# Scatters without fills between them, and a denser timetable, in the first layer of a two-layer graph transformer

## The chip, the cores and the metric

The kernel runs on one core of a Trainium2 chip. The metric is the device time of one launch in microseconds, the median of several runs. The profile shows one execution, taken by the hardware profiler. The core's engines work side by side, each through its own instructions in order: TensorE (PE, with its weight loads PEld), VectorE (DVE), ScalarE (ACT), GpSimd (POOL) and SyncE (SP, which here issues transfers).

## The reference, cut to what matters

Two layers, each a graph part, an attention part and an expert part, on 3125 nodes of 256 features with 50,000 edges sorted by `dst`. Everything is float32. The change lies in layer 0; the graph part of layer 0 is

```python
def _L0_gnn_ref(input, edge_index, edge_weight, weight, bias):
    support = jnp.matmul(input, weight)
    row, col = (edge_index[0], edge_index[1])
    msgs = support[col] * edge_weight[:, None]
    output = jax.ops.segment_sum(msgs, row, num_segments=input.shape[0])
    return output + bias
...
xn = _layernorm(x, axis=-1)
x = x + _L0_gnn_ref(xn, edge_index, edge_weight, ...) + _L0_mix_ref(xn[None], ...)[0]
x = x + _L0_ffn_ref(_layernorm(x, axis=-1)[None], ...)[0]
```

`_L0_mix_ref` is a linear attention over all nodes. `_L0_ffn_ref` sends each node through a shared network and through two of eight experts, which the largest two of eight router values choose. Layer 1 ends in an expert part whose weights come from a second graph, 2048 rows with 32,768 edges; the kernel sorts those edges by their second end, and half of that sort is done during layer 0.

## The kernel before

**The graph part as a matrix.** The kernel doesn't gather rows per edge. It builds a dense weighted adjacency matrix in the chip's main memory (tile `adj`, 25 blocks of 128 rows, one row per `dst`, and 3200 columns, one per `src`, float32) and multiplies it on TensorE with the supports `sup`. Building it takes three steps:
- *Fills of zeros* (`fill`, L471): 25 transfers of 1.6 MB from SP.
- *Chunks* (`edge_chunk`, L384 to L426): the edges come in 16 chunks of 8, 12, ten times 32, 16, 16, 12 and 7 lots; a lot is 128 edges, one per partition. On DVE a chunk adds up weights of edges that fall on one place and works out each edge's place (`ch_code`, `ch_same`, `ch_prod`, `ch_sum`, `ch_place`).
- *Scatters* (`edge_scatter`, L438): one indirect transfer from POOL per lot, 391 in all, 128 single floats each.

**The runs.** Six runs of adjacency matmuls (L599; `RUNS`, blocks 0-3, 4-7, 8-11, 12-15, 16-19, 20-22) each go over 14 groups of columns of `gT`, with 4 or 3 blocks each; DVE adds the result to `gT` (L605; in the first run ACT copies it, L603). SP loads a run's blocks (`load`, L568), in two halves; a load waits until the lots of its edges have landed and until the buffer of the run before is free. Then gT is transposed and added to `x` (L624, L627), and the last two blocks (`CLOSING`, L643, L646) are multiplied chunk by chunk of nodes, beside the moments of the next layer norm (L228 to L239), its rows on ACT (L243), their transposes (L250) and the router's product (L281).

**The sort.** DVE, ACT and PE work on the second graph's sort beside all this (`sort_by_low`): first a ranking by digits (L1344 to L1393), then 256 *columns*: for each, DVE and ACT make selection matrices (`s_hot`, `we`/`wc`/`wi`, `s_z`: L1456 to L1468) and PE multiplies them (L1484, L1489). Where they stand in the engines' order is up to the layer's program: two per group of a run (`ranked(2)`), any number in the pauses of `until`, and what is left is spread evenly over the 27 steps of the transposes and the closing blocks (`columns`).

**The timetable.** PE, DVE, ACT and SP run in the order in which the program writes their instructions. That order comes from a clock of the program's own, `now`, which `advance(us)` moves on by estimates. Three places read it:

```python
yield RATE * (ENDS[c] + (ENDS[c + 1] - ENDS[c]) * i / STEPS) / 128 - AHEAD   # a chunk's step is due
while self.pending and (22.0 + PACE * self.released - LEAD <= until or ...)  # a lot is handed to POOL
ready = 38.0 + RATE * min(16 * (b0 + n) + 4, NJ)                             # a run may start
until(ready)                                                                 # until then: columns of the sort
```

`RATE` (L59) and `PACE` (L60) are the microseconds that the timetable gives to a lot. A lot that is handed over waits for the latest instruction of the tokens or runs at that place in the program (`self.mark`).

**The scatters on POOL.** `spaced` (L294) puts the scatters into one order: each scatter of an edge lot, and later each of the 50 scatters of the expert part's rows into `slots` (L1127), comes behind a `memset` of a small tile `idle` (L298), which itself comes behind the scatter before it. Nothing reads `idle`. `turn_on_queue` states an order on POOL's queue alone, without a semaphore of its own.

Of the kernel before, what the change touches and what calls it, by code (L numbers as in the profile page):

```python
# [9 lines left out]
F32 = mybir.dt.float32  # L10
# [45 lines left out]
SW = 264  # L56
STEPS = 5
AHEAD = 90.0
RATE = 1.38  # L59
PACE, LEAD = 1.48, 78.0  # L60


E2, EC = 32768, 256
# [17 lines left out]
def scatter(nc, table, idx, rows, add=False):  # L81
    kw = {"compute_op": OP.add} if add else {}
    return nc.gpsimd.indirect_dma_start(  # L83
        out=table, out_offset=bass.IndirectOffsetOnAxis(ap=idx, axis=0),
        in_=rows, in_offset=None, **kw)


def pieces_of(c):

    return min(NT, (ENDS[c + 1] + DRIFT) // (16 * P) + 1)  # L90
# [11 lines left out]
def held(t):  # L102

    return P if t < NT - 1 else REST
# [31 lines left out]
class Kernel:  # L136
# [8 lines left out]
    def constants(self):  # L145
        nc, a, c = self.nc, self.a, self.const
        self.x = c.tile([P, NT, D], F32, name="x")
        nc.vector.memset(self.x[:, NT - 1, :], 0.0)
        self.ident = c.tile([128, 128], F32, name="ident")
        make_identity(nc, self.ident)  # L150

        self.above = c.tile([128, 128], F32, name="above")
        nc.gpsimd.memset(self.above, 1.0)
        nc.gpsimd.affine_select(out=self.above, in_=self.above, compare_op=OP.is_gt, fill=0.0,
                                base=0, pattern=[[1, 128]], channel_multiplier=-1)
        self.full = c.tile([128, 128], F32, name="full")
        nc.vector.memset(self.full, 1.0)

        self.node = c.tile([128, EC], F32, name="node")
        nc.gpsimd.iota(self.node, pattern=[[1, EC]], base=0, channel_multiplier=0,  # L160
                       allow_small_or_imprecise_dtypes=True)
        self.real = c.tile([128, 1], F32, name="real")
        nc.gpsimd.memset(self.real, 1.0)
        nc.gpsimd.affine_select(out=self.real, in_=self.real, compare_op=OP.is_gt, fill=0.0,
                                base=REST, pattern=[[0, 1]], channel_multiplier=-1)
        self.idle = c.tile([128, 128], F32, name="idle")
        self.spacer = None
        self.eps = c.tile([128, 1], F32, name="eps")
        nc.vector.memset(self.eps, LN_EPS)

# [120 lines left out]
        self.tc.add_manual_dep(ins.ins, name, mybir.DependencyInfo(  # L291
            mybir.DependencyClass.NoSync, mybir.DependencyReason.DATA), reason="turns on the queue")

    def spaced(self, ins):  # L294

        if self.spacer is not None:
            self.turn_on_queue(ins, self.spacer)
        rest = self.nc.gpsimd.memset(self.idle, 0.0)  # L298
        self.turn_on_queue(rest, ins.ins.name)
        self.spacer = rest.ins.name  # L300
        return ins

    def unordered(self, group, ins):
# [134 lines left out]
    def edge_scatter(self, c, place, wsum, f):  # L438

        ready = pieces_of(c)  # L440
        ins = self.spaced(scatter(self.nc, self.adj[:], place[:, f:f + 1], wsum[:, f:f + 1]))
        for i in range(ready):
            self.after(ins, self.fills[i], "zeros below")
        self.tc.declare_no_dep(ins.ins, group="adj read", reason="blocks that are complete")
        for i in range(ready, NT):
            self.tc.declare_no_dep(ins.ins, group=f"zeros {i}", reason="rows behind the chunk's")
        for i in range(c + 1):
            self.tc.declare_no_dep(ins.ins, group=f"edges {i}", reason="places of their own")
        self.tc.add_to_no_dep_group(f"edges {c}", ins.ins)
        self.edge_scatters.setdefault(c, []).append(ins.ins)  # L450
        return ins


    def layer0(self):
        nc, tc, a = self.nc, self.tc, self.a
        with ExitStack() as c:
# [43 lines left out]
            def chunks():  # L500
                for c in range(len(WIDTHS)):
                    steps = self.edge_chunk(ed, c)
                    for i in range(STEPS):
                        yield RATE * (ENDS[c] + (ENDS[c + 1] - ENDS[c]) * i / STEPS) / 128 - AHEAD
                        next(steps, None)
# [73 lines left out]
            def until(us):  # L579
                while now < us:  # L580
                    advance(next(sort, 1.0))

            turn = 0
            for b0, n in RUNS:
                ready = 38.0 + RATE * min(16 * (b0 + n) + 4, NJ)
                until(ready)
# [337 lines left out]
    def layer0_ffn(self, arrive, far, sorting):  # L924
        nc, tc, a = self.nc, self.tc, self.a
        NE, FC = 8, 8
        SB = BLK // 128
        with ExitStack() as c:
# [5 lines left out]
            rows = rp.enter_context(tc.tile_pool(name="f0r", bufs=1)).tile([P, NT, SW], F32, name="rows")  # L934
# [77 lines left out]
            def routes():  # L1012
# [95 lines left out]
                abi = big.tile([P, 2, NT], I32, name="abi")  # L1108
# [15 lines left out]
                for t in range(NT):  # L1124
                    p = held(t)
                    for i in range(2):
                        self.unordered("slots", self.spaced(scatter(nc, self.slots[:], abi[:p, i, t:t + 1], rows[:p, t, :])))  # L1127

            kp = c.enter_context(tc.tile_pool(name="f0k", bufs=1))
            ranks = self.sort_by_high(kp, hp) if sorting else iter(())  # L1130
            steps = chain(routes(), self.segments(kp) if sorting else (), ranks)
            output(*first_hidden)
            pending = second_hidden
# [17 lines left out]
            def block_in(b):  # L1151
                n = lots(b)
                e = nc.sync.value_load(exi[0:1, b:b + 1], min_val=0, max_val=NE - 1)
                w1 = wa.tile([128, 2, FC * 128], F32, name="w1")
                b1 = wp.tile([128, FC], F32, name="b1", bufs=3)
                b2 = wp.tile([128, D], F32, name="b2r", bufs=3)
                r = wp.tile([128, SB, SW], F32, name="srow", bufs=3)
                nc.sync.dma_start(r[:, :n, :], self.slots[slot(b):slot(b) + 128 * n, :].rearrange("(i p) w -> p i w", p=128))
                nc.sync.dma_start(w1, a["L0_ffn_W1p"][bass.ds(e, 1)].rearrange("o (k p) f -> p (o k) f", p=128))
                nc.sync.dma_start(b1, self.b1p[bass.ds(e, 1)].rearrange("o p f -> p (o f)"))  # L1160
                nc.sync.dma_start(b2, self.b2[bass.ds(e, 1)].to_broadcast([128, D]))
                return e, w1, b1, b2, r
# [67 lines left out]
            ins = {b: block_in(b) for b in T[:2]}  # L1230
# [1454 lines left out]
```

## Time and profile before

| what | value |
|---|---|
| median of 3 runs | 2459.14 us (2455.91 to 2460.01) |
| the profiled execution | 2454.27 us, span 2452.5 us |
| mean granted clock of TensorE | 0.901 |
| busy: PE, DVE, ACT, POOL | 2001.3, 1472.7, 835.4, 1562.2 us |
| edge scatters (L83, `adj`) | 391, 416.4 us, mean 1065 ns |
| slot scatters (L83, `slots`) | 50, 58.9 us, mean 1178 ns |
| memsets of `idle` (L298) | 441, 99.2 us, mean 225 ns |
| adjacency matmuls (L599 into `pb` and `pc`) | 484 and 160 records, 195.6 and 65.6 us |

The span is the time from the first to the last instruction; the time of the launch is 1.8 us longer. The profiled execution is 4.9 us below the median. Busy times say how much an engine did, not whether others waited for it; a share of the whole span mixes stretches with different limits, and layer 0's graph part takes only the first 755 us of it. Idle time in a row is charged to what ended the wait.

### The profile page before, as it was taken

What the parts mean: (1) busy time and instruction counts of PE and PEld (TensorE: products, weight loads), DVE (VectorE), ACT (ScalarE), POOL (GpSimd) and SP (SyncE); (2) the same over time, 40 slices, a digit from 0 to 9 for tenths busy, and PEclk for the clock granted to TensorE, in tenths of its full rate; (3) what the DMA queues carried; (4) which work ended last, traced back from release to release, by engine and by line L of the source; (5) the groups of instructions that cost most, each with busy time, mean ns of one, the idle gap of its engine ahead of it and who ended that gap; (6) DMA issues with size and microseconds to landing.
All of it is one profiled execution on the core that took longest, in us unless ns stands there. A gap on an engine that the chain in (4) does not pass through costs nothing.

```text
span 2452.5 us, 27755 instructions
## 1 busy us (share of the span) xinstructions
PE 2001.3 (82%) x8319; PEld 1415.0 (58%) x8319; DVE 1472.7 (60%) x3952; ACT 835.4 (34%) x1852; POOL 1562.2 (64%) x1924
## 2 busy tenths in 40 slices
PE   1666699899889989899999547777769779999955
PEld 0444355445555668789999435545546566677634
DVE  6888948986823696122222458898886962233346
ACT  1353144564513112333434323444430142222314
POOL 5888888886000562777777157777776437777742
PEclk9985799899957999999999779999989869999977
DMA  8613538223001125677887432222222112113242
GB/s 270 225 57 111 223 137 273 71 100 108 12 1 35 66 82 171 205 256 245 261 258 239 130 82 55 57 54 56 55 60 47 34 28 38 28 21 81 58 140 68
DMA packets 200603, 275.75 MB, mean 112 GB/s; under 512 B 58562, under 2 KB 159415, under 8 KB 200443
## 3 DMA queue, kind: packets, MB, share of 16 engines
q1 hardware_dynamic: 146815, 224.49, 27.4%
q0 software_dynamic: 48480, 44.59, 8.8%
q10 hardware_dynamic: 5148, 4.80, 0.7%
q8 instruction: 68, 1.11, 0.2%
q14 instruction: 92, 0.75, 0.1%
HBM read 195.35 MB, written 78.42 MB: 112 GB/s over the span
## 4 chain that ended last, share of the span: by engine, by line
PE 59%; DVE 24%; issue 5%; ACT 5%; DMA 5%; POOL 2%; ACTq 0%; DVEq 0%; SPq 0%; POOLq 0%
PE pb L1207 8%; PE pb L599 7%; PE pc L1219 7%; PE fph L1987 7%; PE fpy L2003 7%; DVE v L1748 3%; PE pc L599 3%; PE pw L1754 2%; PE pb L972 2%; PE pc L985 2%; PE pb L281 2%; PE pb L643 2%; DMA g<-tab,t_src 1%; POOL g L76 1%; PE pc L1484 1%
## 5 line engine op out<-in xcount | busy, mean ns | idle before, releaser
L76 POOL DMA_INDIRECT g<-tab,t_src x391 | 377.3, 965 | 198.1 <-issue 151.1
L83 POOL DMA_INDIRECT adj<-ch_sum,ch_place x391 | 416.4, 1065 | 91.9 <-issue 54.3
L83 POOL DMA_INDIRECT sorted<-src,pos x256 | 245.2, 958 | 134.9 <-issue 102.1
L76 POOL DMA_INDIRECT G<-tabg,g_src x256 | 256.9, 1003 | 78.0 <-DMA G<-tabg,g_src 39.3
L1754 PE MATMUL pw<-v,hot 128*128 128x260 f32 x782 | 215.1, 436 | 0.0
L1207 PE MATMUL pb<-xs,w 128*128 128x128 f32 (+1 forms) x1248 | 205.5, 324 | 9.2 <-issue 8.6
L599 PE MATMUL pb<-adj,sup 128*128 128x448 f32 (+1 forms) x484 | 195.6, 549 | 15.1 <-DVE r_tot L1354 13.6
L1207 PEld LDWEIGHTS pb<-xs,w 128*128 128x128 f32 x1248 | 187.7, 194 | 25.8 <-issue 9.6
L1219 PE MATMUL pc<-w,h 128*128 128x256 f32 x896 | 199.7, 379 | 0.0
L1209 ACT ACTIVATE h<-pb,b 128x128 f32<-128x128 f32 (+1 forms) x312 | 129.1, 414 | 176.2 <-PE pb L1207 106.9
L1754 PEld LDWEIGHTS pw<-v,hot 128*128 128x128 f32 x782 | 165.7, 217 | 30.0
L1219 PEld LDWEIGHTS pc<-w,h 128*128 128x128 f32 x896 | 167.3, 190 | 21.2
L2003 PE MATMUL fpy<-fw,fh 128*128 128x256 f32 (+1 forms) x800 | 177.7, 379 | 0.0
L1987 PE MATMUL fph<-xT,fw 128*128 128x512 f32 (+2 forms) x448 | 174.1, 542 | 0.0
L83 POOL DMA_INDIRECT slots<-rows,abi x50 | 58.9, 1178 | 177.8 <-DVE abi L1110 167.9
L2003 PEld LDWEIGHTS fpy<-fw,fh 128*128 128x128 f32 (+1 forms) x800 | 149.6, 187 | 31.8 <-issue 8.5
L1466 ACT ACTIVATE s_z<-s_y,s_val 128x128 f16<-128x128 f16 x256 | 112.4, 486 | 122.6 <-issue 108.2
L1989 ACT ACTIVATE fh<-fph,cols 128x512 f32<-128x512 f32 (+2 forms) x112 | 70.2, 633 | 215.6 <-PE fph L1987 215.6
L599 PEld LDWEIGHTS pb<-adj,sup 128*128 128x128 f32 x484 | 90.0, 193 | 91.8 <-issue 85.5
L1987 PEld LDWEIGHTS fph<-xT,fw 128*128 128x128 f32 x448 | 85.3, 191 | 76.0 <-issue 54.9
L1748 DVE TENSOR_TENSOR v<-msg,own_bank 128x2048 f32<-128x2048 f32 (+2 forms) x50 | 111.9, 2239 | 1.7
L298 POOL MEMSET idle<- 128x128 f32 x441 | 99.2, 225 | 0.3
(591 smaller groups left out, 3674.9 us busy)
## 6 DMA issues: line engine op xcount, KB each, us to landing
adj<-zero SPq DMA_DIRECT2D x25, 1600.0 KB
w<-in_L_ffn_W1p_dram SPq DMA_DIRECT2D x39, 1024.0 KB
w<-in_L_ffn_W2p_dram SPq DMA_DIRECT2D x39, 1024.0 KB
adj<-adj SPq DMA_DIRECT2D x24, 896.0 KB
adj<-adj SPq DMA_DIRECT2D x24, 704.0 KB
slots<-empty SPq DMA_DIRECT2D x1, 7392.0 KB
adj<-ch_sum,ch_place POOLq DMA_INDIRECT x391
g<-tab,t_src POOLq DMA_INDIRECT x391
```

The source lines that it names most:

```text
L76: return nc.gpsimd.indirect_dma_start(out=out, out_offset=None, in_=table, in_offset=bass.IndirectOffsetOnAxis(ap=idx, axis=0))
L83: return nc.gpsimd.indirect_dma_start(out=table, out_offset=bass.IndirectOffsetOnAxis(ap=idx, axis=0), in_=rows, in_offset=None, **kw)
L298: rest = self.nc.gpsimd.memset(self.idle, 0.0)
L599: nc.tensor.matmul(pm[:, :w], sup[:, b, k * 128:(k + 1) * 128], mats[b, h][:, c0 - PARTS[h][0]:c0 - PARTS[h][0] + w], start=(b == b0), sto ...
L1207: nc.tensor.matmul(ph[:, :m], w1[:, k, f * 128:(f + 1) * 128], xs[:, k, :m], start=(k == 0), stop=(k == 1))
L1209: ins = nc.scalar.activation(h[:, f, :m], ph[:, :m], AF.Gelu, bias=b1[:, f:f + 1])
L1219: nc.tensor.matmul(py, h[:, f, i * 128:(i + 1) * 128], w2[:, f, :], start=(f == 0), stop=(f == FC - 1))
L1466: nc.scalar.activation(z[:, i, k, :], y, AF.Relu, bias=val[:, k, s], scale=val[:, 2 + k, s])
L1748: self.latest = nc.vector.tensor_mul(v[:, :n, :, :HD], o[:, :n, None, :HD].to_broadcast([128, n, 4, HD]), weight[:, :n, :, None].to_broadc ...
L1754: nc.tensor.matmul(pw.rearrange("p h c -> p (h c)"), hot[:, k, :], v[:, k, :, :].rearrange("p h c -> p (h c)"), start=(k == 0), stop=(k == ...
L1987: nc.tensor.matmul(ph[:, :m], w1[:, k, f * 128:(f + 1) * 128], xT[:, k, t0 * P:t0 * P + m], start=(k == 0), stop=(k == 1))
L2003: nc.tensor.matmul(py[:p], hs[:, f, i * P:i * P + p], w2[:, f, :], start=(f == 0), stop=(f == FC - 1))
```

## The change

`spaced` becomes `in_turn`: the scatters keep the same order, each behind the one before it, but no `memset` stands between them. The tile `idle` goes. `RATE` falls from 1.38 to 1.22 and `PACE` from 1.48 to 1.27. Line numbers below the edit fall by up to three.

```diff
-RATE = 1.38
-PACE, LEAD = 1.48, 78.0
+RATE = 1.22
+PACE, LEAD = 1.27, 78.0
...
-        self.idle = c.tile([128, 128], F32, name="idle")
-        self.spacer = None
+        self.last_lot = None
...
-    def spaced(self, ins):
-
-        if self.spacer is not None:
-            self.turn_on_queue(ins, self.spacer)
-        rest = self.nc.gpsimd.memset(self.idle, 0.0)
-        self.turn_on_queue(rest, ins.ins.name)
-        self.spacer = rest.ins.name
+    def in_turn(self, ins):
+
+        if self.last_lot is not None:
+            self.turn_on_queue(ins, self.last_lot)
+        self.last_lot = ins.ins.name
         return ins
...
-        ins = self.spaced(scatter(self.nc, self.adj[:], place[:, f:f + 1], wsum[:, f:f + 1]))
+        ins = self.in_turn(scatter(self.nc, self.adj[:], place[:, f:f + 1], wsum[:, f:f + 1]))
...
-                        self.unordered("slots", self.spaced(scatter(nc, self.slots[:], abi[:p, i, t:t + 1], rows[:p, t, :])))
+                        self.unordered("slots", self.in_turn(scatter(nc, self.slots[:], abi[:p, i, t:t + 1], rows[:p, t, :])))
```

## The prediction, made before the changed kernel was run

> **What bounds the kernel now.** I read the page first, then the stretches of layer 0 by time, POOL's timeline, the chain of waits, and last the two programs' instruction orders, a listing without times. On the page:
>
> ```profile
> span 2452.5 us, 27755 instructions
> ...
> PE 2001.3 (82%) x8319; PEld 1415.0 (58%) x8319; DVE 1472.7 (60%) x3952; ACT 835.4 (34%) x1852; POOL 1562.2 (64%) x1924
> ...
> POOL 5888888886000562777777157777776437777742
> PEclk9985799899957999999999779999989869999977
> ```
>
> A digit of the last two rows is 61 us. POOL is dense until 600 us and then empty until 822: that is the edge scatters' end. Nothing there waits for it directly, so I cut layer 0 into stretches (columns: PE, PEld, DVE, ACT, POOL busy; PEclk, DMA share, GB/s):
>
> ```profile
> 424.70:459.30 34.60, 24.19 (x163) 12.45 (x161) 34.49 (x127) 30.64 (x79) 31.10 (x42) 0.86 0.31 112
> 511.80:541.90 30.10, 25.64 (x169) 13.41 (x167) 30.06 (x127) 28.78 (x74) 26.77 (x41) 1.00 0.37 128
> ...
> 631.20:655.40 24.20, 18.56 (x146) 12.92 (x145) 24.19 (x85) 16.10 (x41) 2.31 (x7) 1.00 0.04 13
> 655.40:674.40 19.00, 16.60 (x82) 8.84 (x80) 17.91 (x71) 7.21 (x19) 0.00 (x0) 1.00 0.00 0
> 674.40:755.20 80.80, 64.86 (x219) 44.19 (x220) 18.77 (x60) 15.79 (x34) 0.00 (x0) 0.53 0.08 26
> ```
>
> The first two are the pauses of `until(ready)` ahead of runs 3 and 4 (numbered from 0): DVE is full, making sort columns, while the adjacency matmuls stand still. The third is the transposes of gT, full on DVE too. The last is the closing blocks: DVE busy 18.8 of 80.8 us, TensorE at a granted 0.53. This loop sets its pace (chain of waits):
>
> ```profile
> 676.53 0.48 ACT xT L952
> ...
> 677.05 3.58 PE pc L281 x16
> 680.63 4.50 PE pb L643 x8
> 685.13 0.54 PE pc L1484 x2
> 685.67 4.32 PE pb L643 x8
> ...
> 690.01 0.69 DVE x L646
> ```
>
> After 690.01 come the moments on DVE and the rows on ACT, and at 695.98 L281 again: one lap in 18.9 us. Whatever DVE does between L646 and the moments lengthens the lap.
>
> **The fills.** With and, further on, without one behind it, a scatter looks so on POOL:
>
> ```profile
> 519.80 0.96 POOL L83 DMA_INDIRECT adj<-ch_sum,ch_place  x1 [0.17 <-issue]
> 520.77 0.22 POOL L298 MEMSET idle<- 128x128 f32 x1
> 521.15 0.96 POOL L83 DMA_INDIRECT adj<-ch_sum,ch_place  x1 [0.17 <-DVE wc L1459]
> ...
> 1107.59 0.96 POOL L83 DMA_INDIRECT sorted<-src,pos  x1 [0.30 <-issue]
> 1108.85 0.96 POOL L83 DMA_INDIRECT sorted<-src,pos  x1 [0.30 <-ACT h L1209]
> ```
>
> The step is 1.35 us with the fill and 1.26 without: the fill's 0.22 goes, the gap grows from 0.17 to 0.30, and 0.09 is won, not the 0.39 that fill and gap take. From 39.8 us on 383 lots went in 559 us, 1.46 each, because many scatters last longer than 0.96. So I expect about 1.37, against a timetable that drops by 0.16 (RATE) and 0.21 (PACE). The 391st lot ends at 599.1 - 383 x 0.09 = 565. Lot 340, the last that run 4 needs, ended at 524.1 (counted along POOL's timeline); 332 x 0.09 = 30 us less is 494. The longer scatters sit in the pauses:
>
> ```profile
> L83 POOL DMA_INDIRECT adj<-ch_sum,ch_place x21 | 26.4, 1256 | 3.5 <-issue 1.3 <-DVE s_z L1468 0.8 <-DVE wi L1459 0.5
> ...
> L83 POOL DMA_INDIRECT adj<-ch_sum,ch_place x38 | 38.2, 1004 | 7.3 <-issue 4.4 <-DVE s_z L1468 1.0 <-DVE wc L1459 0.5
> ```
>
> The upper row is the first pause (424.7 to 459.3), the lower one run 3 (459.3 to 511.8): 1256 ns beside sort columns, 1004 beside matmuls. If the pauses go, the lots keep closer to 1.27 and lot 340 comes up to 9 us sooner, at 485. I take 490. The Trainium skill, SBUF — State Buffer, "Who interferes with whom", says that a VectorE instruction in a two-port mode and GpSimd exclude each other for a whole instruction; it speaks against a table set at 1.27, and for lots that quicken once the columns are moved behind them. By it alone lot 340 would be at 485, by the row's mean at 494; the sum below would shift by no more than 5 us.
>
> The slot scatters (L1127, 822 to 902 us) win 50 x 0.09 = 4.5 us on POOL. What ends last there is DVE's d_cum chain, which runs to 915 and lets PE go on; I cost this edit at 0 to -2.
>
> **The timetable.** `ready` is 38 + RATE x (16 x blocks + 4): for runs 3, 4 and 5 it falls from 396, 485 and 551 to 355, 433 and 492. Counting the sort columns (10 DVE instructions for four) between the runs in the two orders:
> - pause before run 3: 53 before, 2 after; before run 4: 51 and 15; before run 5: 12 and 2;
> - transposes: 26 and 76; closing: 12 and 62.
>
> So 100 columns leave the pauses and come back behind the runs. Four take 2.34 us on DVE (519.80 onwards, L1456 to L1468 repeating), 0.586 each.
>
> *Runs.* Run 2 ended at 424.7. In the new order one chunk of 32 lots more (10 us of DVE: L402 3.4, L407 1.5, L411 1.5, L418 2.7, small ones 1) stands ahead of run 1. DVE idled 12.6 us there, at 317.8 "<-PE pb L599", and some of the token stage is full, so I take +5. Run 3 starts at 430 instead of 459.3, lasts 51, then 13 columns beyond the running ones at 0.586 are 7.6: 489. The loads of run 4 wait on SP for lot 340 (490); the rest of SP's queue, the other loads of that run, stands behind it but is needed eight groups later. Its transfer takes some 4 us more, and three of four blocks are there already, so run 4 starts at about 494 instead of 537.9, 44 us sooner. Run 4 to the end of run 5 took 537.9 to 631.2; the 3.4 us before run 5 (587.6 to 591.0) go as well. The runs end at 584: -47.
>
> *Transposes.* They are full on DVE, so 50 more columns cost 50 x 0.573 (2.29 for four there) = +29.
>
> *Closing, first three laps* (655.4 to 674.4, 6.3 us each): DVE will have two additions 1.3, some 10 columns 5.9, moments 2.9, together 10.1. Three are 30.3 instead of 19.0: +11.
>
> *Closing, the other laps.* Each gets about 10 columns. The first five run while PE is at the second L643 (685.17 to 690.01 on DVE); but PE has five columns' matmuls ahead of it, 2.5 us cold where it now has 0.6. The second five, 3.0 us, stand between L646 and the moments and nothing covers them. With a cold clock a lap grows by 2.4 + 3.0, and three of them with the last, shorter one come to +21. If the column matmuls bring the clock back within the lap, as 3.4 us of them alone did in the first pause (granted 0.50 in 432.7 to 436.1, 1.00 after it), the second L643 falls from 4.5 to 2.4 us (at 655.4 it took 2.48), and the first part vanishes: +10. I take +15, nearer to the row's 0.53.
>
> Sum: -47 + 29 + 11 + 15 = +8 us. The profiled execution had a span of 2452.5 and a time of 2454.3; that is 4.8 below the median of 2459.1. Added to the median: **2467**.
>
> **Rivals.**
> *The tail swallows the columns.* DVE idles 62 of the last 80.8 us, ACT 65, and the clock is half. If enough column matmuls between the L643 keep it at 1.0, as in 463 to 674 where they stood too, L643 gets 2 x 2.1 us a lap and L281 1.8 cheaper: three laps win 18, the last laps some 6, against +15 for longer warm work: -9 instead of +15. Sum -16: 2443. Against it: from 677.0 to 692.2 PE was busy for 15.15 us of 15.20, with L281, L643 and few columns, and the granted clock stayed at 0.50. The skill's TensorE: Matmul & The Clock Gate, Part 1, lets an idle window of about 3.4 us halve the clock and a busy one restore it; the lap's wait of 3.8 to 5 us for ACT agrees with the first half; the 15 us of busy PE at 0.50 do not with the second. By that rule the sum would be this rival's.
>
> *The lots do not keep up.* Slower still: PE and DVE wait in order for lot 340, and no sort column is left in front to fill the wait. It decides from a step of (489 - 40) / 332 = 1.35 us upwards; every 0.01 costs 3.3 us. At 1.46, if transfers and not POOL set the step, run 4 starts where it did, the 55 us of moved columns are paid in full, and the time is about 2510. Against it: the unspaced scatters at 1107 step by 1.26, with 128 elements of 4 bytes too. At 1.40, run 4 is 17 us later: 2484.
>
> *A draw.* Gains and returns cancel: each column costs the same wherever it stands, and the sum of -47 and +40 before the last laps leaves -7; with +10 for those it is +3, within 0.2%, 4.9 us, about what a measurement here can tell from no change.
>
> **How the numbers follow.** Forecast (slower by some 5 to 20) 0.42, lots too slow 0.09, draw 0.2, the tail swallows them 0.29. The range takes most of the warm tail (2443, with 4 us either way) and the cold one at a step of 1.38: 2446 to 2485; what lies outside is the warmest tail and a step over 1.4. Faster 0.29, same 0.2, slower 0.51.
>
> **What would show it.** In the new profile: scatters of `adj` in a step of 1.27 to 1.40, the last at 555 to 570; the first L627 near 586 (before 633.4); the transposes some 52 us long; the laps at L646 of 21 to 24 us; no long wait at L599 for `adj<-adj`. Wrong it is if L599 waits over 10 us before run 4, if the last L599 ends after 600, or if PEclk in the closing is over 0.8.

## The result, and the profile after

The changed kernel takes 2497.16 us (median of 6 runs, 2494.37 to 2502.57) against 2458.20 for the kernel before on the same chip: a ratio of 1.0166, 95% interval 1.0151 to 1.0182. That is 39 us slower, where 8 were forecast. Some of the experiments ran on three chips on which the kernel before takes 2823 to 2837 us; they stand in a section of their own, and everywhere else the kernel before takes 2454 to 2459.

From the page of the changed kernel, the lines that answer to those shown of before, and the group of adjacency matmuls (L599 before, L596 now: busy, mean ns, idle before them and what ended it):

```profile
span 2492.7 us, 27288 instructions
...
PE 2003.8 (80%) x8319; PEld 1418.9 (57%) x8319; DVE 1465.4 (59%) x3952; ACT 835.1 (34%) x1852; POOL 1468.6 (59%) x1483
...
PEclk9986799889966999999999769999988959999977
...
L596 PE MATMUL pb<-adj,sup 128*128 128x448 f32 (+1 forms) x484 | 197.7, 553 | 46.3 <-DMA adj<-adj 46.2
```

PE, DVE and ACT do the work that they did before, POOL 93.6 us less. What is new is in the last line: TensorE stands idle for 46 us ahead of adjacency matmuls, all of it waiting for their blocks. Before, the same line read

```profile
L599 PE MATMUL pb<-adj,sup 128*128 128x448 f32 (+1 forms) x484 | 195.6, 549 | 15.1 <-DVE r_tot L1354 13.6
```

with nothing of it worth naming for loads. By stretches (columns as in the prediction; run 3, run 4, transposes, and the closing from the sixth addition at L643 to the last, which is not the cut of the row 674.40:755.20 in the prediction):

```profile
430.60:495.70 65.10, 52.72 (x196) 27.33 (x195) 34.57 (x112) 16.39 (x42) 49.87 (x51) 0.90 0.29 102
500.70:576.40 75.70, 52.56 (x196) 26.92 (x195) 27.82 (x98) 19.45 (x51) 49.27 (x50) 0.84 0.27 91
...
618.00:668.80 50.80, 40.44 (x291) 24.65 (x288) 50.80 (x205) 45.67 (x119) 1.60 (x6) 0.97 0.02 7
...
690.80:775.30 84.50, 65.79 (x253) 41.70 (x254) 37.17 (x146) 33.97 (x85) 0.00 (x0) 0.60 0.00 1
```

Run 3 starts at 430.6, as forecast (430), and run 4 at 500.7, 37 us sooner than before, where 494 was forecast. But they last 65 and 76 us, where they took 52.5 and 49.8 before, with PE busy for 53 in each. PE's timeline shows where run 4 stops, first before, then in the changed kernel:

```profile
537.77 3.17 PE L599 MATMUL pb<-adj,sup 128*128 128x448 f32 x8
...
500.70 2.42 PE L596 MATMUL pb<-adj,sup 128*128 128x448 f32 x6
526.25 1.86 PE L596 MATMUL pb<-adj,sup 128*128 128x448 f32 x2 [23.14 <-DMA adj<-adj]
```

Six matmuls, for the three blocks that are there, and then 23.14 us for the fourth, block 19; another 12.4 us fall in run 3, for block 15, and 10.7 at the start of the first run. SP's queue (405 to 545 us, before and after) says what its loads wait for (us in total, times, longest):

```profile
SPq L568 <- DMA adj<-ch_sum,ch_place: 52.6, 4, 24.8
...
SPq L565 <- DMA adj<-ch_sum,ch_place: 72.3, 5, 42.1
```

For scatters. Block 19 needs the lots up to the 340th of the source. By POOL's timeline the 340th scatter ended at 499.0, the 356th at 519.3; the load went out at 520.8 (the 340th, the 356th, the load):

```profile
498.08 0.96 POOL L83 DMA_INDIRECT adj<-ch_sum,ch_place  x1 [0.30 <-DVE wi L1456]
...
518.38 0.96 POOL L83 DMA_INDIRECT adj<-ch_sum,ch_place  x1 [0.30 <-issue]
...
520.77 0.32 SPq L565 DMA_DIRECT2D adj<-adj  x1
```

Block 15 needs 276 lots; the 276th scatter ended at 414.5 and the load went out at 440.3. Before, either load followed its scatter within 1.5 us (427.4 and 428.8, 524.1 and 525.5). The 340th scatter comes 25 us sooner than before (9 us later than the forecast's 490), and the loads are 22 to 26 us behind their scatters.

**Where the 22 us are.** The instruction order holds the answer, in the semaphore values that a load waits for. Counted in the order in which the scatters stand on POOL's queue, the last one that each load waits for is

```text
load of block    before    changed kernel
13                  244               264
15                  276               294
17                  308               322
19                  340               356
20                  356               370
```

The scatters don't go out in the order of the source any more. The 32 lots of the chunk that holds lots 245 to 276 stand at places 235 to 294, mixed with those of the chunks around it. The loads of blocks 15 and 19 go out 1.5 and 1.4 us behind the 294th scatter (438.8) and the 356th. So the change did not do what its description says, "in the same order". That `in_turn` asks for the order and doesn't get it has a likely reason, argued and not tried by itself: `edge_scatter` also declares that a lot depends on no lot of its own or an earlier chunk, and an order stated between two lots goes with that dependence. The memset was in none of those groups, and the chain of scatter, memset, scatter held. Which lots get overtaken was not traced.

### The profile page after: what moved, and what is told of

Same layout as the page of the kernel before. It is cut to its first block, busy times and chain, and to the rows that moved or that the text cites. A ratio compares the mean times of both kernels' runs of the same rounds, so it can differ in the third digit from the quotient of the medians.

```text
span 2492.7 us, 27288 instructions
## 1 busy us (share of the span) xinstructions
PE 2003.8 (80%) x8319; PEld 1418.9 (57%) x8319; DVE 1465.4 (59%) x3952; ACT 835.1 (34%) x1852; POOL 1468.6 (59%) x1483
## 4 chain that ended last, share of the span: by engine, by line
PE 55%; DVE 25%; DMA 7%; issue 5%; ACT 5%; POOL 3%; SPq 0%; DVEq 0%; ACTq 0%; POOLq 0%
PE pb L1204 8%; PE pc L1216 7%; PE pb L596 7%; PE fph L1984 6%; PE fpy L2000 6%; DVE v L1745 3%; PE pc L982 3%; PE pw L1751 2%; PE pb L969 2%; PE pc L596 2%; PE pc L1481 1%; DMA G<-tabg,g_src 1%; POOL g L76 1%; DVE s_z L1465 1%; DMA g<-tab,t_src 1%
## 5 line engine op out<-in xcount | busy, mean ns | idle before, releaser
L83 POOL DMA_INDIRECT adj<-ch_sum,ch_place x391 | 416.4, 1065 | 144.6 <-issue 102.7
L596 PE MATMUL pb<-adj,sup 128*128 128x448 f32 (+1 forms) x484 | 197.7, 553 | 46.3 <-DMA adj<-adj 46.2
L596 PEld LDWEIGHTS pb<-adj,sup 128*128 128x128 f32 x484 | 90.5, 195 | 124.0 <-issue 80.5
L1173 DVE COPY xs<-pa 128x256 f32<-128x256 f32 (+1 forms) x39 | 21.0, 538 | 124.1 <-PE pa L1172 124.0
```

The costliest lines, as they stand in the source:

```text
L83: return nc.gpsimd.indirect_dma_start(out=table, out_offset=bass.IndirectOffsetOnAxis(ap=idx, axis=0), in_=rows, in_offset=None, **kw)
L596: nc.tensor.matmul(pm[:, :w], sup[:, b, k * 128:(k + 1) * 128], mats[b, h][:, c0 - PARTS[h][0]:c0 - PARTS[h][0] + w], start=(b == b0), sto ...
```

## The experiments

Theory A: the lost order makes the loads wait for 14 to 20 scatters too many, and the runs lose to it most of the 32 us by which they end later than forecast (616.4, not 584). Theory B: the scatters' or the loads' transfers land late, behind the fill of `slots` and other traffic.

### The order kept, without the memsets' time

A memset of one column behind every fourth scatter, tied to the four before it and the four after:

```diff
-        self.last_lot = None
+        self.last_lot, self.lots = None, []
+        self.idle = c.tile([128, 1], F32, name="idle")
...
         if self.last_lot is not None:
             self.turn_on_queue(ins, self.last_lot)
-        self.last_lot = ins.ins.name
+        self.lots.append(ins.ins.name)
+        if len(self.lots) == 4:
+            rest = self.nc.gpsimd.memset(self.idle, 0.0)
+            for name in self.lots:
+                self.turn_on_queue(rest, name)
+            self.last_lot, self.lots = rest.ins.name, []
         return ins
```

Expected:

> The kernel of e1_order_kept a third time, for a chip on which the kernel before takes the 2458 us of the first profile. Theory A (order of the lots lost): the loads of blocks 15 and 19 go out within 3 us of the 276th and the 340th scatter, PE waits for adjacency loads at most 15 us instead of 46, the runs end at 582 to 592, time 2462 to 2475. Theory B (transfers late): the loads stay 15 us or more behind, time 2492 to 2502. If the kernel before takes over 2800 us again, only the distance between load and scatter is read from this run.

Measured: 2473.87 us (2470.90 to 2479.51), before 2453.72 on that chip, ratio 1.0090 (1.0069 to 1.0110). SP's queue in the same stretch, PE's timeline at run 4 (lines are six further down), and the group of the page:

```profile
SPq L571 <- DMA adj<-ch_sum,ch_place: 44.2, 3, 26.5
```

```profile
489.57 2.42 PE L602 MATMUL pb<-adj,sup 128*128 128x448 f32 x6
503.30 1.86 PE L602 MATMUL pb<-adj,sup 128*128 128x448 f32 x2 [11.30 <-DMA adj<-adj]
```

```profile
L602 PE MATMUL pb<-adj,sup 128*128 128x448 f32 (+1 forms) x484 | 198.0, 554 | 22.3 <-DMA adj<-adj 22.3
```

The waits of PE for blocks fall by 24 us, from 46.2 to 22.3, and so does the time, by 23 (by 19, if each is set against the kernel before on its own chip). The 15 us that were expected at most are missed: 11.3 are run 4's, and 10.8 lie at the start of the first run, as in the changed kernel. The scatters themselves are no different: the 340th ends at 496.7 (499.0 without the order), the last at 562.9 (564.9), and block 19's load goes out at 498.1, 1.4 us behind its scatter. Block 15's load, at 418.4, is 5.9 us behind its scatter and not within the 3 that were expected, but it is its turn on SP that sets this: the run's loads begin at 414.5, about 1.3 us each. The runs end at 593.3, 1.3 us above the expected range. Theory A holds for 23 of the 32 us. B falls: the edit leaves the transfers as they were.

### The dense timetable alone

The kernel before, memsets and all, at 1.22 and 1.27.

> The kernel of h1_fills_dense again (the dense timetable alone, memset of 128x128 behind every scatter, order kept), for a chip on which the kernel before takes its 2457 us. Theory A: the 340th scatter ends at 522 to 530, block 19's load follows within 3 us, run 4 works from about 529, run 5 ends at 615 to 624, and the time is 2494 to 2506: the timetable alone costs what the whole change does. Rival C (the lots' step is not what the runs wait for): 2470 to 2480.

Measured: 2506.50 us (2502.75 to 2508.35), ratio 1.0197 (1.0179 to 1.0215), 0.5 us above the expected range. The 340th scatter ends at 524.3, the load follows at 525.7, and run 4 waits:

```profile
497.77 2.42 PE L599 MATMUL pb<-adj,sup 128*128 128x448 f32 x6
531.19 1.86 PE L599 MATMUL pb<-adj,sup 128*128 128x448 f32 x2 [31.00 <-DMA adj<-adj]
```

The runs end at 621.4. So a timetable denser than the scatters costs 47 us (2506.5 less 2459.4 before on that chip), by itself and with the order kept. Taking the memsets out brings the 340th scatter from 524.3 to 496.7, 27.6 us for 332 scatters or 0.083 each (0.09 forecast), and the order lost with them gives 23 us of the gain back at the end of the runs (616.4 against 593.3).

### The memsets alone

The changed kernel at the old 1.38 and 1.48; the order is lost here too (block 15 waits for the 280th scatter, block 19 for the 349th).

> The kernel of h2_nofill_old again (memsets gone, order lost, old timetable), for a chip on which the kernel before takes its 2458 us. Theory A: 2446 to 2456, since the pauses hide the lost order. Rival D (the lost order costs its 23 us under any timetable): 2474 to 2482. A third reading, from the three chips on which the kernel before took 2823 to 2837 and this one 3.0 to 3.7% more: scatters without a pause between them hold up the other engines, over 2480.

Measured: 2454.50 us (12 runs, 2451.36 to 2459.87), before 2457.14, ratio 0.9989 (0.9978 to 1.0001): no difference that can be told. The two pauses are as full as before and as long, 34.8 and 26.6 us against 34.6 and 26.1 (the prediction's row of the second, 511.8 to 541.9, holds the first 4 us of run 4 as well):

```profile
427.90:462.70 34.80, 24.57 (x163) 12.41 (x160) 34.61 (x126) 30.56 (x79) 26.20 (x23) 0.82 0.28 105
513.80:540.40 26.60, 21.86 (x155) 11.33 (x153) 26.60 (x110) 25.43 (x66) 20.50 (x21) 0.94 0.42 145
```

Block 19's load goes out at 520.4, 1.4 us behind the 349th scatter and 13 us behind the 340th, and nobody waits for it, since the pause's columns run until 540.4. Scatters that end 25 us sooner (574.4 against 599.1) are worth nothing while the columns set the pauses' length, and a lost order costs nothing there either: no matmul of the runs waits for a block in this profile.

### Columns where PE is full and DVE is not

The order kept, 1.26 and 1.31 (37 columns in the pause before run 4 and not 15), and four columns behind each group of runs 4 and 5:

```diff
-RATE = 1.22
-PACE, LEAD = 1.27, 78.0
+RATE = 1.26
+PACE, LEAD = 1.31, 78.0
...
-                        ranked(2)
+                        ranked(4 if b0 >= 16 else 2)
```

> The kernel of h4_pause4_runs again (order kept by a small memset behind every fourth scatter, 1.26 and 1.31, four columns behind each group in runs 4 and 5). On the slower chip it stood 17 us below the same without the extra columns in the runs: 52 columns there lengthened runs 4 and 5 by 16 us, 0.32 each, and shortened transposes and closing by 33. Theory A now: 2474 less 12 for PE's wait in run 4 less 17: 2441 to 2452. Rival E (the wait in run 4 stays): 2454 to 2462.

Measured: 2444.70 us (10 runs), ratio 0.9951 (0.9934 to 0.9969), faster than both kernels. Runs 4, 5 and the transposes:

```profile
500.00:559.50 59.50, 58.15 (x272) 31.75 (x270) 42.52 (x162) 34.94 (x90) 47.26 (x58) 1.00 0.33 114
560.60:608.00 47.40, 47.40 (x244) 26.47 (x242) 39.69 (x152) 31.99 (x83) 2.30 (x3) 1.00 0.20 76
608.00:641.60 33.60, 25.24 (x185) 16.74 (x184) 31.93 (x119) 25.46 (x65) 1.64 (x7) 0.90 0.03 10
```

Run 4 waits for block 19 for 1.4 us now. Before, runs 4 and 5 took 49.8 and 40.2; 52 more columns made them 15.5 longer beside that wait, 0.30 each. In the changed kernel's transposes 50 more cost 28.1 us, 0.56 each. In the runs PE is the full engine (47.40 of 47.40 in run 5), and a column costs about what its matmuls take, 0.34: on PE's timeline eight take 1.05 us and the four of `s_hot` 0.30, for four columns. What the two edits of this kernel bring one by one was not measured on such a chip.

With five columns behind each group (65 in each of the two runs):

> As i2_pause4_runs, with five sort columns behind each group of runs 4 and 5 instead of four (65 each instead of 52; transposes 23 instead of 37, closing 6 instead of 20). By the price of a column in the runs, PE 0.34 (eight matmuls 1.05 and four more 0.30 for four columns), and DVE not yet full there (38 of 55): 26 columns cost 9 us in the runs, and spare 14 times 0.57 and 14 times 0.6 in transposes and closing, 16 us: 2434 to 2442 against its 2444.7. If DVE becomes the full engine in the runs: 2444 to 2452.

Measured: 2441.53 us (2439.55 to 2446.21), ratio 0.9928 (0.9915 to 0.9942), the lowest here, though its interval overlaps that of four columns.

```profile
568.10:619.60 51.50, 51.50 (x282) 29.61 (x281) 47.61 (x187) 39.48 (x102) 0.00 (x0) 1.00 0.18 69
```

DVE is busy for 47.61 of 51.50 us in run 5 then. Whether more columns still pay was not tried.

### The same kernels on three slower chips

Four of the kernels also ran on two chips on which the kernel before takes 2837 and 2824 us, and two of them on a third (2823), with two steps towards the best version. Each chip was used in one sitting, so whether it is the chip or its state at the time isn't shown.

> As the changed kernel, dense timetable and all, but behind every fourth scatter stands one memset of a single column (128x1), which the four scatters before it and the four after it are tied to, so that the lots go out in the order of the source again, to within four. Theory A (the order of the lots was lost: in the instruction order the load of block 15 waits for the 294th scatter on the queue instead of the 276th, that of block 19 for the 356th instead of the 340th, and that costs the runs some 32 us): the load of block 15 goes out within 3 us of the 276th scatter, that of block 19 within 3 us of the 340th, PE waits for adjacency loads at most 15 us instead of 46, run 4 starts near 500 minus 4 for the slower scatters it no longer waits for, the runs end at 582 to 592 instead of 616, and the time is 2462 to 2475. Theory B (the loads go late because the scatters' transfers land late behind the fill of the slots and the other transfers): the loads stay 15 us or more behind the 276th and the 340th scatter, and the time stays within 5 us of the changed kernel's 2497.

> The kernel before with its memset of 128x128 behind every scatter, and only the dense timetable (1.22 and 1.27). The order of the lots is held by the memsets. Theory A: the lots keep their old step, the 340th ends near 524, run 4 starts near 530, the runs end at 615 to 622, the transposes and the closing take the moved columns as in the changed kernel (+28 and +28), and the time is 2494 to 2506, about that of the changed kernel: taking out the memsets brought it nothing, since the lost order gave the gain back. Theory B: scatters without memsets gain what they can, so this kernel is slower than the changed one by 10 us or more, 2507 to 2515.

> The changed kernel with the old timetable (1.38 and 1.48): only the memsets are gone, and with them the order of the lots (block 15 waits for the 280th scatter on the queue, block 17 for the 326th, block 19 for the 349th). The sort columns stay in the pauses. Theory A: the pauses are as long as their columns, the lost order is hidden behind these, and the time is 2448 to 2460, that of the kernel before to within 5 us or a little less; L596 waits for adjacency loads under 10 us. Theory B says the same as long as transfers keep under the pauses: 2448 to 2465. A third reading, that the memsets' removal itself slows the kernel (scatters crowd DVE or the queues), gives over 2470.

> The old timetable, no memset behind each scatter, and the small memset behind every fourth, which keeps the order. Theory A: as with the order lost, the pauses are set by their columns: 2448 to 2460, within 3 us of the kernel that lost the order under the old timetable. If the faster lots alone were worth something, it would be below 2450. Theory B: no different from the run that lost the order either.

On the second chip, the same four:

> The kernel of e1_order_kept once more, since on that chip the kernel before took 2837 us and no transfer stretch passed 220 GB/s where the first profile had 410. The numbers are as before. Theory A (order of the lots lost): the loads of blocks 15 and 19 go out within 3 us of the 276th and the 340th scatter, PE waits for adjacency loads at most 15 us, the runs end at 582 to 592, time 2462 to 2475. Theory B (transfers late): the loads stay 15 us or more behind, time 2492 to 2502.

> The kernel of e2_fills_dense once more (all memsets, dense timetable). Theory A: 340th scatter near 524, run 4 from near 530, runs end at 615 to 622, time 2494 to 2506. Theory B: 2507 to 2515.

> The kernel of e3_nofill_old once more (no memsets, order lost, old timetable). Theory A: the pauses hide the lost order, 2448 to 2460. Theory B: 2448 to 2465. If the memsets' removal itself slows the kernel, as the slow chip suggests (1.037 there), over 2470.

> The kernel of e4_kept_old once more (small memset behind every fourth scatter, order kept, old timetable). Theory A and B: 2448 to 2460, within 3 us of the kernel that lost the order under this timetable; over 2470 if scatters without memsets slow the rest, as the slow chip suggests (1.024 there).

And on the third:

> The dense timetable alone: the kernel before with its memset of 128x128 behind every scatter (order kept, slow step) and 1.22 and 1.27. Theory A (the changed kernel's runs lose 23 us to the lost order, shown by the run that kept it, 2474; the memsets are worth some 25 us to the lots): the 340th scatter ends at 522 to 530, block 19's load follows within 3 us, run 4 works from about 529 to 580, run 5 ends at 615 to 624, and with the tail of the changed kernel the time is 2494 to 2506. So the memsets' removal and the lost order cancel. Rival C (the lots' step is not what the runs wait for): 2470 to 2480, as with the order kept.

> The memsets' removal alone, order lost, old timetable (1.38 and 1.48). Theory A: the lost order costs only where PE would wait for it; here the pauses are full of sort columns until 459 and 538, the 280th and the 349th scatter on the queue come by about 420 and 512, so nothing is seen of it: 2446 to 2456, that of the kernel before less 0 to 8 us. Rival D (the lost order costs its 23 us under any timetable): 2474 to 2482.

> The kernel that kept the order (small memset behind every fourth scatter), at 1.26 and 1.31: in the instruction order the pause before run 4 has 37 sort columns instead of 15, that before run 3 has 4 instead of 2, and transposes and closing have 65 and 48 instead of 75 and 62. Theory A: the 22 more columns fill the 11.3 us that PE waited for block 19 in the run that kept the order, and leave the tail at 0.57 us each (12.5 us): 2458 to 2466 against its 2474. Rival E (the 11.3 us are filled by something else by then, or the lots come later with the slower table): 2470 to 2478.

> As h3_pause4, and runs 4 and 5 take four sort columns behind each group instead of two (52 columns each instead of 26; transposes and closing 37 and 20). PE is the full engine in the runs (50.00 busy of 50.00 in run 4 of before), DVE is half idle; a column costs PE about 0.47 us by the longer transposes (23.7 us more PE time for 50 columns). Theory A: 52 columns at 0.47 in the runs instead of 0.57 and 0.45 in the tail, 0 to 8 us less than h3_pause4: 2452 to 2464. Rival F (DVE's idle time in the runs takes them for nothing): 2436 to 2444, and the kernel would beat both.

The times expected there have no meaning on these chips. The ratios to the kernel before on the same chip:

| kernel | before at 2454 to 2459 | 2837 | 2824 | 2823 |
|---|---|---|---|---|
| memset behind each scatter, dense | 1.0197 | 1.0134 | 1.0164 | 1.0138 |
| memset behind each 4th, dense | 1.0090 | 1.0408 | 1.0360 | |
| no memsets, old timetable | 0.9989 | 1.0374 | 1.0326 | 1.0300 |
| memset behind each 4th, old timetable | | 1.0236 | 1.0217 | |
| memset behind each 4th, 1.26 and 1.31 | | | | 1.0366 |
| the same, four columns in runs 4 and 5 | 0.9951 | | | 1.0303 |

The intervals are 0.1 to 0.6 points either way. The order of the rows turns round: on these chips it is the memsets' removal that costs, 3.0 to 3.7% under the old timetable with the order lost, 2.2 to 2.4% with the order kept by the small memsets (these two were expected within 3 us of each other, and lie 35 and 24 apart). How the chips differ shows in one kernel (memsets, dense timetable) on both kinds, in the stretch in which the experts' weights stream in; first a chip of the usual kind, then the third:

```profile
990.00:1394.00 404.00, 394.70 (x2205) 356.29 (x2204) 105.07 (x471) 153.67 (x365) 291.35 (x304) 0.99 0.76 242
```

```profile
1052.00:1554.00 502.00, 419.46 (x2206) 374.39 (x2205) 104.19 (x465) 149.89 (x365) 293.58 (x307) 0.93 0.64 196
```

About the same bytes at 196 GB/s and not 242. But the transfers themselves are hardly slower: their engines are busy for 0.64 of the longer stretch and 0.76 of the shorter, 321 and 307 us. Over the whole program the main queue's packets take 27.0% of 2501.0 us and 24.0% of 2855.4, 675 and 685 (the two pages, in the same order):

```profile
q1 hardware_dynamic: 146815, 224.49, 27.0%
...
q1 hardware_dynamic: 146815, 224.49, 24.0%
```

What differs is waits that the profile charges to nothing on the core ("issue" and "remote"). Added up over these two profiles (gaps of over 0.15 us), DVE stands in them for 0.4 us on the usual chip and 542 on the third, TensorE for 9 and 197. In the other profiles it is the same, with and without memsets: 542 to 701 us of DVE on the three chips, at most 2 on the usual ones. (That transfers are slower was read, in the expectation for the second chip, by setting 410 GB/s against 220; slices as long as those of the page reach 273 in the kernel before and 290 in the run that it speaks of.)

From 100 to 200 us, in the token stage, TensorE's waits without memsets (first) and with them, both on the third chip:

```profile
PE pb L280 <- issue: 47.3, 2, 30.6
```

```profile
PE pb L281 <- issue: 9.3, 4, 3.4
```

Waits of up to 31 us. The first run starts at 363.5 us without memsets, at 302.5 with them; on the usual chips these two start at 269.6 and 273.6. Their timetables differ too, but pairs on one chip under one timetable say the same. On the first two chips the dense timetable has the first run start at 321.1 and 329.4 with a memset behind each scatter, at 365.0 and 361.0 with one behind each fourth; under the old timetable it starts at 339.3 and 344.3 with one behind each fourth, at 361.6 and 361.5 with none. So more pauses between scatters go with an earlier first run there; what the engines wait for stays open. One pair agrees with the price above: on the third chip four columns in runs 4 and 5 lengthened these by 16 us and shortened transposes and closing by 32; the time fell by 17 us, where 0 to 8 were expected.

## Why the prediction was right or wrong

Its sum, against the changed kernel and the one that kept the order (profiled executions; the run that ended the matmuls of L599, the first L646, and the start of L972 are the cuts; the closing's own cut is the end of the third lap's moments, 674.4 before and 697.0 after):

| step | forecast | changed kernel | order kept |
|---|---|---|---|
| end of the runs | -47 | -14.8 (616.4) | -37.9 (593.3) |
| transposes, up to the first L646 | +29 | +28.1 | +28.1 |
| closing, first three laps | +11 | +9.3 | |
| closing, the other laps | +15 | +19.0 | |
| closing, all laps together | +26 | +28.3 | +28.2 |
| after it, slots among it | 0 to -2 | -1.4 | -1.8 |
| sum | +8 | +40.2 | +16.7 |

**The step that failed** is "the loads of run 4 wait on SP for lot 340 (490)". They wait for the 356th scatter on the queue. The forecast counted lots and took it for granted that the queue holds them in that order. Among its rivals it had none in which the change doesn't do what it says, though the instruction order showed it in advance. 23 of the 32 us lie there. The other 9 are a size: the 340th scatter came at 496.7 and not at 490, and its block was there 6.6 us later and not 4. The row's mean step of 1.37 gave 494; the forecast went below it on the word of the longer scatters in the pauses.

**Scatters.** The last ended at 564.9 (forecast 565), in a step of 1.26 where nothing lies between, at a gap of 0.30. But "if the pauses go, the lots keep closer to 1.27" did not come: the mean of all 391 is 1065 ns in both kernels. In run 3 they took 996 ns, as the 1004 of before; elsewhere others got longer. The Trainium skill, SBUF — State Buffer, "Who interferes with whom", was weighed there for lots that quicken with the columns gone; the whole gives no such gain.

Of the prediction's three signs of being wrong two came: 23 us of wait ahead of run 4, and runs that end at 616 and not before 600.

**Transposes** were right within 1 us. The **closing** was within 2.3 (26 against 28.3) partly by luck: its first three laps were put 2 too high and the others 4 too low. Its cold end (+21) was nearer for these others than the +15 taken: a lap shows both parts that were forecast (chain of waits, from the first L640 on), though three laps grew by 3.8, 5.8 and 4.1 us and not by 5.4 each:

```profile
703.25 4.50 PE pb L640 x8
707.75 1.82 PE pc L1481 x8
709.57 0.34 PE pc L1486 x4
709.91 0.54 PE pc L1481 x2
710.45 3.01 PE pb L640 x8
713.48 0.69 DVE x L643
```

PE does five columns, 2.70 us, between the two L640, and after L643 DVE makes columns up to 717.10, where the moments begin. The clock came back for 6.8 us from 711.8 on, which is why the second L640 took 3.01 and not 4.50, and then fell to 0.50 again; over these laps it is 0.60, and the **warm tail**, the rival at 2443, is out. The Trainium skill, TensorE: Matmul & The Clock Gate, Part 1, lets one busy window bring the clock back: here 13.4 us of full PE, 700.0 to 713.4, had a mean of 0.56, so the rule doesn't carry over to this loop.

**The lots do not keep up** was the rival that came nearest, at 2484 to 2510: PE and DVE wait in order, with no column in front to fill the wait. What this rival puts down to the step was mostly the order; with the order kept, the step to the 340th scatter was 1.376, and the 9 us over the point of 1.35 are what this rival asks for (3.3 us for 0.01). The range, up to 2485, took this case in only up to a step of 1.40.

**One price for a column** wherever it stands, on which the draw rested, was wrong for the runs: 0.30 there, 0.56 in the transposes. The forecast needed no column moved into the runs, and so lost nothing by it; the best version lives on it. The pauses were no idle time of TensorE either: of the first it was busy for 24.19 of 34.60 us, of the second for 21.64 of 26.10, with the columns' matmuls. Those have to be done somewhere. Three readings were slightly off, and nothing hangs on them: the row of the second pause takes in 4 us of run 4, run 3 was put at 51 us where the trace of before has 52.5 (it took 50.8 with the order kept), and of the 100 columns that come back behind the runs, 97 come from the three pauses listed.

## What to carry to other kernels

An order that a program asks for is worth what the built queue shows: where consumers count completions, read the count that each one waits for, in the instruction order, before pricing what a faster queue brings. A timetable is denser than its producer only at the price of waits with nothing in front, so a pause full of needed work is no gain to be had by closing it. Work that can stand in several places is priced by the engine that is full in each of them.

## What was not expected of the hardware

- Taking the memsets from between the scatters, old timetable, cost nothing on a chip where the kernel before takes 2457 us (0.9989) and 3.0 to 3.7% on three chips where it takes 2823 to 2837. A memset of 0.22 us behind each of them was cheap cover there; why is open.
- On those three chips DVE stands for 542 to 701 us in waits that have no name, on the usual ones for 2 at most, while the main queue's packets take about the same time (675 and 685 us). So a lower GB/s is not by itself a slower transfer, and which of two edits wins on one chip can turn round on another.
